# LoRA layer stack on one core: last layers split by token halves, down-weight sums in three steps

## Chip, cores and metric

The kernel runs on one core of one Trainium2 chip. The metric is the time of one execution on the device in microseconds (us); of several executions the median counts. Engines are named as in the profile: PE is TensorE's matrix multiply, PEld its weight load, DVE is VectorE, ACT ScalarE, POOL GpSimd, SP SyncE. A name such as "SPq" means that the engine only issues a DMA there. L446 is line 446 of the kernel before.

## What is computed

Four layers follow one another, each added to its own input. All numbers are fp32; x has 8 x 256 tokens of width 1024.

```python
x = x + L0(x)   # x W^T + b + 2 * (x A^T) B, one adapter for each sequence, rank 16
x = x + L1(x)   # down(silu(gate(x)) * up(x)), hidden width 2752; gate, up and down
                # each add 0.5 * (input A^T) B^T of the sequence's adapter, rank 16
x = x + L2(x)   # (x B^T) A^T, one adapter for each sequence, rank 16
x = x + L3(x)   # (x B^T) A^T, one adapter for each sequence, rank 16
```

The adapters are picked by index inputs, so their tables are gathered by indirect DMAs. L2 and L3 have no dense product. They are computed together here: their two rank-16 products are one "shrink" to ranks and one "expand" back.

## The kernel before

**Layout.** x is held transposed: 1024 features down the partitions, in 8 chunks of 128 (`NC`), and 2048 tokens across. Tokens are worked on in two blocks (`blk` 0 and 1) of 1024, and each block in two halves of 512 (`n` = 0 and 1).

**Products.** A dense product is cut into 2 x 2 blocks and computed by seven products instead of eight (Winograd's form of Strassen's method, `ORDER` 1, 2, 3, 5, 6, 7, 4). In gate, up and the first part of down this is done at two levels. The price is sums: of weights (four for a 2 x 2 set) and of tokens, made by POOL and DVE, and of results, added by DVE out of PSUM. A 128 x 512 fp32 matmul is recorded as two passes.

**Order.** The program is a list of `Unit`s; a unit is one of the outer seven products (or one column of layer 0 or of down). A unit calls `at(slot)` between its inner products. Whatever has been hooked to that slot is emitted there, and after it pieces of a `beside` queue up to a share in cost. A scheduler then keeps for each engine the order so made, as far as data allow. So "slot 4 of unit 2" is a place in every engine's queue.

**Stages.** Layer 0 runs for block 0 and then for block 1. Then each block runs gate and up (`gate_up`), the down projection and the last layers.

- *Layer 0* (units of `job(o)`, four for a block): `sum_w(o)` lets DVE make four sums of the weights (`weight_sums`, L366 to L369) in slot 3 of the unit before. Results are added by DVE with the bias (`with_bias`, L841) and without (`more`, L846).
- *gate_up*: a group `g` of hidden columns is a `Quads` of seven units. POOL makes the outer sums (`outer`, L437) and, a unit ahead, the inner sums `sw` (`inner_sums`, L446 to L449). DVE adds each result bank (`first` L507, `more` L510, and `whole` L519, which adds two SBUF operands). Tokens `tk` are loaded on SP from `toks` a unit ahead (L425).
- *Sums of down weights*: `sum_down(c)` (L755 to L766) treats one of eight pieces of the down weights: load on POOL's DMA queue into `wo` (L759), four POOL sums in place (L761 to L764), four stores to `wsum` in DRAM on POOL's queue (L766). Piece 0 is emitted in block 1's third unit of layer 0 (slot 6), pieces 1 and 2 in the fourth (slot 0), pieces 3 to 7 in block 0's gate_up, in units 2 and 5 of each group (slot 4).
- *Down*: first a `Quads`-like part that reads `wsum`, then four units `2_{blk}_{o}`, whose `job` makes products 1, 5, 6, 3, 2, 7 and leaves product 4 in `pending`, to be emitted by the next `flush()`. DVE adds each to the result `x2` (L1268).
- *Last layers*: `shrink23` multiplies two feature chunks of `x2` as they get ready by the gathered tables `b2` and `b3`. There are four column groups of 32 (`r`, two for a token half and two for the layers), all into one PSUM bank `p23`; `shrink_into` is L261. When the last two chunks are in, `rank_out` (L254) scales and masks the bank into `t`, `expand` (L276) multiplies `t` by `a23`, 64 rows for a token half, and an add puts the result on `x2` (L1392). In block 1, for the chunks in `TAIL` and the second half, ACT copies the bank to `spare` and POOL adds it (L1390). The result is stored (L1396).

**PSUM.** The pools are `ps_a` (2 banks), `ps_b` and `ps_c` (1 each) and `ps_l` (4).

Of the kernel before, what the change touches and what calls it, by code (L numbers as in the profile page):

```python
# [8 lines left out]
F32 = mybir.dt.float32  # L9
# [4 lines left out]
P = 128  # L14
D = 1024
NC = D // P
HC = NC // 2
# [5 lines left out]
TB = 1024  # L23
BB = TB // S
NBLK = NB * S // TB
NN = TB // 512
# [21 lines left out]
TAIL = (0, 2, 4, 6)  # L48
# [6 lines left out]
def kernel(  # L55
# [48 lines left out]
    nc = tc.nc  # L104
# [146 lines left out]
    def rank_out(ps, scale, name):  # L251

        t = tpool.tile([P, 512], F32, tag="t", name=name)
        nc.vector.scalar_tensor_tensor(t, ps, scale, mask, op0=ALU.mult, op1=ALU.mult)  # L254
# [19 lines left out]
    def expand(ps, b, i, t, lo, hi, start=False):  # L274

        nc.tensor.matmul(  # L276
            ps,
            b[lo:hi, i * P : (i + 1) * P],
            t[lo:hi, :],
            start=start,  # L280
            stop=True,
            skip_group_check=True,
        )

    def copy(dst, src, scale=1.0):
        nc.scalar.activation(dst, src, AF.Identity, scale=scale)  # L286
# [6 lines left out]
    class Unit:  # L293


        def __init__(self, name, emit, share):
            self.name, self.emit, self.share = name, emit, share
            self.ahead = []
            units.append(self)
# [5 lines left out]
        def at(self, slot, f):  # L305
            self.ahead.append((0, slot, f))
# [50 lines left out]
    def flush():  # L357
        while pending:
            pending.pop(0)()
# [12 lines left out]
    def product(ps, w, moving, j, start=False):  # L372

        for k, (v, m) in enumerate(zip(w, moving)):
            nc.tensor.matmul(  # L375
                ps,
                v[j],
                m[j],
                start=start and k == 0,
                stop=k == len(moving) - 1,  # L380
                skip_group_check=True,
            )


    class Quads:
# [366 lines left out]
    ]  # L752
    wsum = dram.tile([4, P, 2 * BIG], F32, tag="wsum", name="wsum")

    def sum_down(c):  # L755

        t = big(f"wo_{c}").rearrange("p (j c) -> p j c", j=4)
        cols = slice(c * 512, (c + 1) * 512)
        nc.gpsimd.dma_start(out=t, in_=wd2[:, :, cols].rearrange("j p c -> p j c"))  # L759
        a11, a12, a21, a22 = (t[:, j] for j in range(4))  # L760
        nc.gpsimd.tensor_add(a22, a21, a22)  # L761
        nc.gpsimd.tensor_sub(a21, a11, a21)
        nc.gpsimd.tensor_sub(a11, a22, a11)
        nc.gpsimd.tensor_sub(a12, a12, a11)  # L764
        for j, x in enumerate((a22, a11, a21, a12)):
            nc.gpsimd.dma_start(out=wsum[j, :, cols], in_=x)  # L766

    sts = [{} for _ in range(NBLK)]
    arrival = [c + h for c in range(HC) for h in (0, HC)]
# [2 lines left out]
    def layer0(blk):  # L772
# [149 lines left out]
        for i, o in enumerate((0, 2, 1, 3)):  # L922
            if blk == 0 and i == 0:
                u = Unit("0_plain", lambda at, o=o: plain(o, at), 0)
                u.before(1, 0, load_x)
                for c in range(HC):
                    u.before(1, 0, lambda c=c: sum_x(c))
            else:
                u = Unit(f"0_{blk}_{o}", lambda at, o=o: job(o, at), 1.3)
                u.before(1, 0, lambda o=o: load_w(o))  # L930
                u.before(1, 3, lambda o=o: sum_w(o))
                if i == 0:
                    u.before(1, 0, load_x)
                    for c in range(HC):
                        u.before(1, 4 + c // 2, lambda c=c: sum_x(c))
                    u.at(4, first_shrink)
            if i % 2:
                u.at(8, lambda kk=o % 2: finished(kk))
            if blk == 1 and i > 1:
                for c in ((0,), (1, 2))[i - 2]:  # L940
                    u.at((6, 0)[i - 2], lambda c=c: sum_down(c))

    def gate_up(blk):
        st = sts[blk]
# [38 lines left out]
        def job(g):  # L983
# [86 lines left out]
            q = Quads(blk, f"1_{blk}_{g}", 2, raw, done, SHARE)  # L1070
            q.units[0].before(3, 0, lambda: tables(g))
            if blk == 0 and g < KQ:
                for s, c in ((2, 2 * g + 3), (5, 2 * g + 4)):
                    if c < 8:
                        q.units[s].at(4, lambda c=c: sum_down(c))

        def rest():

# [89 lines left out]
    def down_projection(blk):  # L1168
# [93 lines left out]
        def job(o, at):  # L1262
            p = o + HC
            w, moving = st["wt", o], st["hm"]
            n = f"2_{blk}_{o}"

            def more(k, j, ps):
                nc.vector.tensor_add(x2[k][j], x2[k][j], ps)  # L1268

            at(0)  # L1270
            pa, pc = bank(ps_a, f"pa_{n}"), bank(ps_c, f"pc_{n}")
            product(pa, w, moving, 1, True)
            more(o, 0, pa)
            at(1)
            product(pc, w, moving, 5, True)
            more(p, 1, pc)
            at(2)
            flush()
            at(3)
            product(pa, w, moving, 6)  # L1280
            more(o, 1, pa)
            at(4)
            product(pc, w, moving, 3)
            more(o, 1, pc)
            at(5)
            pb = bank(ps_b, f"pb_{n}")
            product(pb, w, moving, 2, True)
            more(o, 0, pb)
            at(6)
            product(pa, w, moving, 7)  # L1290
            more(p, 1, pa)
            at(7)

            def last():
                product(pa, w, moving, 4)
                more(p, 0, pa)

            pending.append(last)
# [49 lines left out]
        def shrink23(chunks):  # L1348

            for mh in range(2):  # L1350
                for n in range(NN):
                    need(("x2", blk, mh, n))
            need(("b3", blk))
            if chunks[0] == 0:
                st["p23"] = bank(ps_l, f"p23_{blk}")
            for c in chunks:
                for r in range(4):
                    shrink_into(
                        st["p23"],
                        r,  # L1360
                        (st["b2"], st["b3"])[r % 2],
                        NC,
                        c,
                        r // 2,
                        st["x2"][c][r // 2],
                        c == 0,
                        c == NC - 1,
                    )

        def table_a():  # L1370
            st["a23"] = gather_b(a23, off_23[:, blk : blk + 1], f"a23_{blk}")

        def last_layers():
            flush()
            x2 = st["x2"]
            shrink23([HC - 1, NC - 1])
            ps = st["p23"]
            t = rank_out(ps, 1.0, f"t23_{blk}")
            late = []
            if blk + 1 == NBLK:  # L1380
                spare = big("spare").rearrange("p (j t) -> p j t", j=4)
            for o in range(NC):
                pss = [bank((ps_l, ps_a)[o % 2], f"p23_{blk}_{o}_{n}") for n in range(NN)]
                for n in range(NN):
                    expand(pss[n], st["a23"], o, t, 64 * n, 64 * n + 64, start=True)
                for n in range(NN):
                    if blk + 1 == NBLK and o in TAIL and n == 1:

                        copy(spare[:, TAIL.index(o)], pss[n])
                        nc.gpsimd.tensor_add(x2[o][n], x2[o][n], spare[:, TAIL.index(o)])  # L1390
                    else:
                        nc.vector.tensor_add(x2[o][n], x2[o][n], pss[n])  # L1392
                    at = blk * TB + n * 512

                    def store(o=o, n=n, at=at):
                        (nc.scalar, nc.sync)[blk + 1 == NBLK].dma_start(  # L1396
                            out=outT[o * P : (o + 1) * P, at : at + 512], in_=x2[o][n]
                        )


                    if blk + 1 < NBLK:
                        beside.append((0.2, store))
                    elif o in TAIL and n == 1:
                        late.append(store)
                    else:
                        store()
            for f in late:
                f()

        def next_tokens(kk):  # L1410

# [185 lines left out]
```

## Time and profile before

| what | us |
|---|---|
| median of 3 runs (lowest, highest) | 1844.57 (1839.25, 1848.33) |
| the profiled execution, its own time | 1823.64 |
| its span in the trace | 1821.8 |
| mean granted TensorE clock in it | 0.993 of full speed |

The profiled execution is shorter than the median of the runs. A sum made from durations of the profile is compared with 1823.64, and then carried over to the median.

The profile's costliest groups of instructions show what the engines do. The columns are line, engine, operation, output and inputs, size and count, then the busy time and the mean of one in ns, then the engine's idle time just before, and what ended most of it:

```profile
L446 POOL TENSOR_TENSOR sw<-w_B 128x512 f32<-128x512 f32 x60 | 76.8, 1280 | 139.1 <-PE pa L476 121.3
...
L437 POOL TENSOR_TENSOR w_B<-w_B,w_B 128x1024 f32<-128x1024 f32 x40 | 93.5, 2361 | 2.4 <-PE pa L476 2.4
```

A POOL sum of 128 x 512 numbers takes 1.28 us, one of 128 x 1024 takes 2.36. The eight pieces of `wo` are listed by tile: operation, count, the durations in ns (lowest, median, highest) and the starts of the first and the last:

```profile
L766 POOL DMA_DIRECT2D wsum<-wo x32: 540/547/575, 186.8 to 523.3; - x32
L759 POOL DMA_DIRECT2D wo<-in_wd_dram x8: 753/782/797, 173.2 to 505.6; - x8
L761 POOL TENSOR_TENSOR wo<-wo x8: 1263/1271/1276, 183.2 to 516.6; 128x512 f32<-128x512 f32 x8
...
  DMA wo<-in_wd_dram: 22.0, 6
```

The last of these lines says how long POOL stood idle, in six of the eight pieces, until the piece's own load had landed. And this is the end of the chain that ended last (start, duration, what):

```profile
1800.67 1.92 PE p L261 x14
1802.59 0.02 issue
1802.61 0.70 DVE t L254
1803.31 0.04 issue
1803.36 2.90 PE p L276 x12
...
1809.41 1.28 POOL c_d_Y L1390
```

The last shrinks end at 1802.6, DVE makes `t`, and the expands begin at 1803.36.

### The profile page before, as it was taken

The page shows a single profiled execution, that of the slowest core. Times are in us where ns is not written, and L with a number is a line of the kernel's source. Part 1 is how long each engine was busy: PE and PEld are TensorE (multiplying, and loading weights), DVE is VectorE, ACT ScalarE, POOL GpSimd, SP SyncE. Part 2 cuts the span into 40 slices and gives each one's busy share as a digit, 9 for nine tenths or more (in the row PEclk, how much of TensorE's full clock was granted, in tenths as well). Part 3 has the DMA queues.
Part 4 walks back from the last instruction along what each step waited for, and adds up shares of the span by engine and source line. Part 5 has one row for each costly group of instructions (what it writes and reads, how often), then busy time and mean ns, then how long its engine had stood idle before and what let it go on. Part 6 is the DMA issues. An engine that isn't in the chain of part 4 may idle for free.

```text
span 1821.8 us, 20670 instructions
## 1 busy us (share of the span) xinstructions
PE 1797.6 (99%) x7664; PEld 1315.5 (72%) x7664; DVE 1073.0 (59%) x1673; ACT 298.9 (16%) x536; POOL 1006.3 (55%) x778
## 2 busy tenths in 40 slices
PE   9999999999999999999999999999999999999997
PEld 4444477878787878788864568888888887888743
DVE  5484355666757575766852474757575658445623
ACT  0121022021111111133210031120202121221000
POOL 6202578887887677353450467676767664443301
PEclk9999999999999999999999999999999999999999
DMA  6477694767575756679941775575757565655302
GB/s 231 177 278 273 216 369 178 295 217 303 207 309 191 270 188 245 220 280 334 325 143 52 268 299 186 180 276 189 271 193 270 191 239 189 242 174 178 118 0 92
DMA packets 115253, 403.37 MB, mean 221 GB/s; under 512 B 11858, under 2 KB 42706, under 8 KB 105682
## 3 DMA queue, kind: packets, MB, share of 16 engines
q1 hardware_dynamic: 100496, 366.51, 55.4%
q0 software_dynamic: 10496, 28.72, 4.6%
q10 hardware_dynamic: 4162, 6.82, 1.2%
q8 instruction: 62, 1.02, 0.2%
q14 instruction: 37, 0.30, 0.0%
HBM read 317.59 MB, written 84.41 MB: 221 GB/s over the span
## 4 chain that ended last, share of the span: by engine, by line
PE 93%; DVE 5%; DMA 1%; issue 1%; POOL 0%; ACT 0%; POOLq 0%; ACTq 0%; DVEq 0%
PE pa L476 26%; PE pc L476 13%; PE pa_d L476 11%; PE pa L375 10%; PE pb L476 6%; PE pc_d L476 5%; PE pc L375 5%; PE pb_d L476 3%; PE pa_r L476 3%; PE pb L375 3%; PE pl L974 2%; PE pc_r L476 1%; PE pd L261 1%; PE pp L866 1%; PE p L261 1%; DVE c_Z L519 1%
## 5 line engine op out<-in xcount | busy, mean ns | idle before, releaser
L476 PE MATMUL pa<-tk,sw 128*128 128x256 f32 x1120 | 269.6, 384 | 1.7 <-DVE c_X L507 1.7
L476 PE MATMUL pc<-tk,sw 128*128 128x256 f32 x1120 | 268.4, 383 | 0.0
L476 PEld LDWEIGHTS pa<-tk,sw 128*128 128x128 f32 x1120 | 209.5, 190 | 58.7 <-issue 13.7
L476 PEld LDWEIGHTS pc<-tk,sw 128*128 128x128 f32 x1120 | 215.1, 192 | 31.6 <-issue 1.0
L476 PE MATMUL pa<-tk,w_B 128*128 128x256 f32 x960 | 228.4, 381 | 1.5 <-DVE c_Y L510 1.5
L476 PEld LDWEIGHTS pa<-tk,w_B 128*128 128x128 f32 x960 | 181.2, 190 | 36.2 <-DVE c_E L507 6.5
L446 POOL TENSOR_TENSOR sw<-w_B 128x512 f32<-128x512 f32 x60 | 76.8, 1280 | 139.1 <-PE pa L476 121.3
L614 POOL TENSOR_TENSOR dx_d<-dw_d 128x1024 f32<-128x1024 f32 x14 | 33.0, 2359 | 163.9 <-PE pa L476 44.3
L476 PE MATMUL pb<-tk,w_B 128*128 128x256 f32 x480 | 113.9, 380 | 0.0
L476 PE MATMUL pa_d<-dh_d,dw_d 128*128 128x256 f32 x448 | 102.2, 379 | 0.0
L476 PE MATMUL pc_d<-dh_d,dw_d 128*128 128x256 f32 x448 | 101.7, 379 | 0.0
L476 PEld LDWEIGHTS pb<-tk,w_B 128*128 128x128 f32 x480 | 91.8, 191 | 12.7
L507 DVE TENSOR_TENSOR c_X<-c_X,pa 128x512 f32<-128x512 f32 x90 | 61.3, 681 | 63.9 <-PE pa L476 63.8
L437 POOL TENSOR_TENSOR w_B<-w_B,w_B 128x1024 f32<-128x1024 f32 x40 | 93.5, 2361 | 2.4 <-PE pa L476 2.4
L476 PEld LDWEIGHTS pa_d<-dh_d,dw_d 128*128 128x128 f32 x448 | 85.0, 190 | 12.4 <-issue 0.8
L476 PEld LDWEIGHTS pc_d<-dh_d,dw_d 128*128 128x128 f32 x448 | 85.0, 190 | 12.4 <-issue 0.8
L448 POOL TENSOR_TENSOR sw<-w_B 128x512 f32<-128x512 f32 x60 | 85.4, 1423 | 0.0
L449 POOL TENSOR_TENSOR sw<-w_B,sw 128x512 f32<-128x512 f32 x60 | 81.6, 1360 | 3.6
L447 POOL TENSOR_TENSOR sw<-sw,w_B 128x512 f32<-128x512 f32 x60 | 78.9, 1315 | 0.0
L286 ACT ACTIVATE c_X<-pa 128x512 f32<-128x512 f32 x30 | 17.8, 592 | 365.0 <-PE pa L476 365.0
L231 POOL DMA_INDIRECT ad<-in_ad_dram,off_a x48 | 46.0, 958 | 29.2 <-PE pd L261 18.6
L375 PE MATMUL pa<-ht,wd 128*128 128x512 f32 x128 | 59.1, 594 | 0.0
(380 smaller groups left out, 3168.9 us busy)
## 6 DMA issues: line engine op xcount, KB each, us to landing
tk<-toks SPq DMA_DIRECT2D x140, 896.0 KB, 6.7
w_B<-in_wgu_dram SPq DMA_DIRECT2D x40, 1024.0 KB, 5.1
tk_r<-toks SPq DMA_DIRECT2D x28, 896.0 KB, 11.4
hk<-c_Z SPq DMA_DIRECT2D x32, 512.0 KB, 4.3
dh_d<-hk SPq DMA_DIRECT2D x14, 1024.0 KB, 9.3
hk<-c_Y SPq DMA_DIRECT2D x24, 512.0 KB, 3.7
x1d<-x SPq DMA_DIRECT2D x8, 1024.0 KB, 6.0
wo<-in_wd_dram POOLq DMA_DIRECT2D x8, 1024.0 KB, 8.3
```

Of the source, the lines that this page charges most:

```text
L231: nc.gpsimd.indirect_dma_start(out=t, out_offset=None, in_=table, in_offset=bass.IndirectOffsetOnAxis(ap=off, axis=0),)
L261: nc.tensor.matmul(ps[32 * r : 32 * r + 32, :], v, src, start=start, stop=stop, skip_group_check=True)
L375: nc.tensor.matmul(ps, v[j], m[j], start=start and k == 0, stop=k == len(moving) - 1, skip_group_check=True,)
L437: f(self.raw[out][:, c], self.raw[a][:, c], self.raw[b][:, c])
L446: nc.gpsimd.tensor_add(s1, m21, m22)
L447: nc.gpsimd.tensor_sub(s2, s1, m11)
L448: nc.gpsimd.tensor_sub(s3, m11, m21)
L449: nc.gpsimd.tensor_sub(s4, m12, s2)
L476: nc.tensor.matmul(ps[:, q, :], w(j, q, kk), tok(j, kk), start=start and q == 0 and kk == 0, stop=kk == self.deep - 1, skip_group_check=True,)
L507: nc.vector.tensor_add(view(out, r, k), view(old, r, k), ps)
L614: nc.gpsimd.tensor_sub(s3, a11, a21)
L974: nc.tensor.matmul(ps[outs], st["bgu", g][rows, table, n, cols], st["t"][rows, table, n, :], start=True, stop=True, skip_group_check=True,)
```

## The change

1. `sum_down` becomes a class with three steps that are hooked separately. Load and stores go to SP's DMA queue; the four sums stay on POOL, with the same arithmetic.
2. The pieces are placed anew. Pieces 0 to 3 are all in the fourth unit of layer 0's block 1, sums in slots 0, 2, 4 and 6, the load two slots ahead and the store three slots behind. Piece g + 4 is in group g (0 to 3) of block 0's gate_up: load in slot 0 and sums in slot 5 of unit 2, stores in slot 0 of unit 4.
3. In down's `job` product 7 is emitted before product 2.
4. The shrink bank `p23` becomes two banks, one for each token half. The last layers of the second half (its last shrinks, ranks and first expand) are emitted before `flush()`, that is before the last unit's product 4 (which `flush()` emits; it changes only the first half). Then the expands alternate between the halves. `rank_out` is replaced here by two multiplies of 64 rows with the mask.
5. In block 1 the four stores that follow POOL's adds go to ACT's DMA queue, the other twelve stay on SP's.

```diff
-    def sum_down(c):
-
-        t = big(f"wo_{c}").rearrange("p (j c) -> p j c", j=4)
-        cols = slice(c * 512, (c + 1) * 512)
-        nc.gpsimd.dma_start(out=t, in_=wd2[:, :, cols].rearrange("j p c -> p j c"))
-        a11, a12, a21, a22 = (t[:, j] for j in range(4))
-        nc.gpsimd.tensor_add(a22, a21, a22)
-        nc.gpsimd.tensor_sub(a21, a11, a21)
-        nc.gpsimd.tensor_sub(a11, a22, a11)
-        nc.gpsimd.tensor_sub(a12, a12, a11)
-        for j, x in enumerate((a22, a11, a21, a12)):
-            nc.gpsimd.dma_start(out=wsum[j, :, cols], in_=x)
+    class SumDown:
+        def __init__(self, c):
+            self.c, self.cols = c, slice(c * 512, (c + 1) * 512)
+        def load(self):
+            self.t = big(f"wo_{self.c}").rearrange("p (j c) -> p j c", j=4)
+            nc.sync.dma_start(out=self.t, in_=wd2[:, :, self.cols].rearrange("j p c -> p j c"))
+        def sums(self):
...
+        def store(self):
+            for j, x in enumerate((3, 0, 2, 1)):
+                nc.sync.dma_start(out=wsum[j, :, self.cols], in_=self.t[:, x])
...
-            if blk == 1 and i > 1:
-                for c in ((0,), (1, 2))[i - 2]:
-                    u.at((6, 0)[i - 2], lambda c=c: sum_down(c))
+            if blk == 1 and i == 3:
+                for c in range(4):
+                    w = SumDown(c)
+                    u.at(2 * c - 2 if c else 0, w.load)
+                    u.at(2 * c, w.sums)
+                    u.at(2 * c + 3, w.store)
...
             if blk == 0 and g < KQ:
-                for s, c in ((2, 2 * g + 3), (5, 2 * g + 4)):
-                    if c < 8:
-                        q.units[s].at(4, lambda c=c: sum_down(c))
+                w = SumDown(g + 4)
+                q.units[2].at(0, w.load)
+                q.units[2].at(5, w.sums)
+                q.units[4].at(0, w.store)
...
+            product(pa, w, moving, 7)
+            more(p, 1, pa)
+            at(6)
             pb = bank(ps_b, f"pb_{n}")
             product(pb, w, moving, 2, True)
             more(o, 0, pb)
-            at(6)
-            product(pa, w, moving, 7)
-            more(p, 1, pa)
             at(7)
...
             for c in chunks:
-                for r in range(4):
-                    shrink_into(
...
+                for n in range(NN):
+                    shrink_half(c, n)
+
+        def shrink_half(c, n):
+            if c == 0:
+                st["p23", n] = bank(ps_l, f"p23_{blk}_{n}")
+            for j, b in enumerate((st["b2"], st["b3"])):
+                shrink_into(
+                    st["p23", n], 2 * n + j, b, NC, c, n, st["x2"][c][n], c == 0, c == NC - 1
+                )
...
+            def ranks(n):
+                rows = slice(64 * n, 64 * n + 64)
+                t[n] = tpool.tile([P, 512], F32, tag="t", name=f"t23_{blk}_{n}")
+                nc.vector.tensor_mul(t[n][rows], st.pop(("p23", n))[rows], mask[rows])
+
+            def store(o, n):
+                at = blk * TB + n * 512
+                queue_of = nc.sync if final and not (n == 1 and o in TAIL) else nc.scalar
+                queue_of.dma_start(out=outT[o * P : (o + 1) * P, at : at + 512], in_=x2[o][n])
+
+            def products(*which):
+                pss = []
+                for o, n in which:
+                    banks.append(None)
+                    ps = bank((ps_l, ps_a)[len(banks) % 2], f"p23_{blk}_{o}_{n}")
+                    expand(ps, st["a23"], o, t[n], 64 * n, 64 * n + 64, start=True)
+                    pss.append(ps)
+                for (o, n), ps in zip(which, pss):
+                    if final and n == 1 and o in TAIL:
+
+                        copy(spare[:, TAIL.index(o)], ps)
+                        nc.gpsimd.tensor_add(x2[o][n], x2[o][n], spare[:, TAIL.index(o)])
+                        late.append((o, n))
+                        continue
+                    nc.vector.tensor_add(x2[o][n], x2[o][n], ps)
...
+            for c in (HC - 1, NC - 1):
+                shrink_half(c, 1)
+            shrink_half(HC - 1, 0)
+            ranks(1)
             flush()
-            x2 = st["x2"]
-            shrink23([HC - 1, NC - 1])
-            ps = st["p23"]
-            t = rank_out(ps, 1.0, f"t23_{blk}")
...
+            products((0, 1))
+            shrink_half(NC - 1, 0)
+            products((1, 1))
+            ranks(0)
+            products((2, 1))
+            for o in range(NC - 3):
+                products((o, 0), (o + 3, 1))
+            for o in range(NC - 3, NC):
+                products((o, 0))
             for f in late:
-                f()
+                store(*f)
```

More of the change, by code (lines that the diff above doesn't have):

```diff
@@ L753 @@
     wsum = dram.tile([4, P, 2 * BIG], F32, tag="wsum", name="wsum")
-    def sum_down(c):
-        t = big(f"wo_{c}").rearrange("p (j c) -> p j c", j=4)
-        cols = slice(c * 512, (c + 1) * 512)
-        nc.gpsimd.dma_start(out=t, in_=wd2[:, :, cols].rearrange("j p c -> p j c"))
-        a11, a12, a21, a22 = (t[:, j] for j in range(4))
-        nc.gpsimd.tensor_add(a22, a21, a22)
-        nc.gpsimd.tensor_sub(a21, a11, a21)
-        nc.gpsimd.tensor_sub(a11, a22, a11)
-        nc.gpsimd.tensor_sub(a12, a12, a11)
-        for j, x in enumerate((a22, a11, a21, a12)):
-            nc.gpsimd.dma_start(out=wsum[j, :, cols], in_=x)
+    class SumDown:
[5 more added lines that the diff above has]
+        def sums(self):
+            a11, a12, a21, a22 = (self.t[:, j] for j in range(4))
+            nc.gpsimd.tensor_add(a22, a21, a22)
+            nc.gpsimd.tensor_sub(a21, a11, a21)
+            nc.gpsimd.tensor_sub(a11, a22, a11)
+            nc.gpsimd.tensor_sub(a12, a12, a11)
+        def store(self):
+            for j, x in enumerate((3, 0, 2, 1)):
+                nc.sync.dma_start(out=wsum[j, :, self.cols], in_=self.t[:, x])
     sts = [{} for _ in range(NBLK)]
@@ L1353, in shrink23 @@
             need(("b3", blk))
-            if chunks[0] == 0:
-                st["p23"] = bank(ps_l, f"p23_{blk}")
             for c in chunks:
-                for r in range(4):
-                    shrink_into(
[L1359 to L1368, printed above, removed]
+                for n in range(NN):
[7 more added lines that the diff above has]
+                )
         def table_a():
@@ L1373, in last_layers @@
         def last_layers():
-            flush()
-            x2 = st["x2"]
-            shrink23([HC - 1, NC - 1])
-            ps = st["p23"]
-            t = rank_out(ps, 1.0, f"t23_{blk}")
[L1379 to L1406, printed above, removed]
@@ new lines, in last_layers @@
+            x2, t, late, banks = st["x2"], {}, [], []
+            final = blk + 1 == NBLK
+            if final:
+                spare = big("spare").rearrange("p (j t) -> p j t", j=4)
+            def ranks(n):
[6 more added lines that the diff above has]
+                queue_of.dma_start(out=outT[o * P : (o + 1) * P, at : at + 512], in_=x2[o][n])
@@ new lines, in products @@
+            def products(*which):
[12 more added lines that the diff above has]
+                    nc.vector.tensor_add(x2[o][n], x2[o][n], ps)
+                    if final:
+                        store(o, n)
+                    else:
+                        beside.append((0.2, lambda o=o, n=n: store(o, n)))
```

## The prediction

> **What bounds the kernel now.** I read the busy times first, then who TensorE waits for, then two windows that run the same program, then single instructions inside them.
>
> ```profile
> span 1821.8 us, 20670 instructions
> PE 1797.6 (99%) x7664; PEld 1315.5 (72%) x7664; DVE 1073.0 (59%) x1673; ACT 298.9 (16%) x536; POOL 1006.3 (55%) x778
> ```
>
> TensorE is the bound: 1821.8 - 1797.6 = 24 us are all that it idles, start and tail included. The change takes no product away, so it can win only from those idle times, from slowed passes, and from the tail. TensorE's list of waits names them:
>
> ```profile
> PE pa L375 <- DVE x L841: 2.9, 1, 2.9
> PE pa L476 <- DVE c_X L507: 1.7, 2, 0.8
> PE pa L476 <- DVE c_X L510: 1.6, 1, 1.6
> PE pa L476 <- DVE c_Y L510: 1.5, 2, 1.0
> ...
> PE p L276 <- DVE t L254: 0.8, 1, 0.8
> ```
>
> All are waits for VectorE. Gate and up run the same program for both blocks, but only block 0 holds five of the eight sum_down pieces. Both windows (busy time of PE, PEld, DVE, ACT, POOL; granted clock; DMA) start and end at the same instructions:
>
> ```profile
> 280.00:568.00 288.00, 283.57 (x1314) 229.47 (x1313) 192.22 (x266) 42.66 (x74) 234.66 (x179) 0.99 0.67 247
> 1076.50:1355.50 279.00, 279.00 (x1314) 227.73 (x1313) 173.37 (x265) 42.74 (x74) 190.05 (x133) 0.99 0.61 217
> ```
>
> Block 0 takes 9 us longer for the same 1314 matmuls; set against the same pd shrink in both blocks (363.08 and 1159.19 us, and so on) the difference is 8.8 us. DVE is busy 19 us longer with one instruction more. The timelines show why: DVE, then POOL, in block 0; then DVE at the same place of block 1.
>
> ```profile
> 361.00 4.11 DVE L519 TENSOR_TENSOR c_Y<-c_Y,c_X 128x512 f32<-128x512 f32 x1
> ```
> ```profile
> 359.74 1.08 POOL L766 DMA_DIRECT2D wsum<-wo  x2
> 360.83 1.28 POOL L446 TENSOR_TENSOR sw<-w_B 128x512 f32<-128x512 f32 x1
> 362.05 1.28 POOL L448 TENSOR_TENSOR sw<-w_B 128x512 f32<-128x512 f32 x1
> 363.27 1.27 POOL L447 TENSOR_TENSOR sw<-sw,w_B 128x512 f32<-128x512 f32 x1
> ```
> ```profile
> 1158.19 0.69 DVE L519 TENSOR_TENSOR c_Y<-c_Y,c_X 128x512 f32<-128x512 f32 x1
> ```
>
> L519 reads two operands from SBUF. It lasts until POOL pauses after three sums: 4.11 instead of 0.69 us. The pa bank is then added late (L507, L510) and TensorE waits. Layer 0 shows the same on block 1's last weights:
>
> ```profile
> 182.60 2.46 DVE L366 TENSOR_TENSOR sw<-w 128x512 f32<-128x512 f32 x1
> 185.10 2.34 DVE L367 TENSOR_TENSOR w<-w 128x512 f32<-128x512 f32 x1
> 187.47 1.75 DVE L368 TENSOR_TENSOR sw<-w 128x512 f32<-128x512 f32 x1
> 189.26 1.74 DVE L369 TENSOR_TENSOR sw<-w,sw 128x512 f32<-128x512 f32 x1
> 190.92 0.74 DVE L841 SCALAR_TENSOR_TENSOR x<-pa,bias,x 128x512 f32<-128x512 f32 x1
> ```
>
> Near 156 to 159 us, with POOL quiet, the same four take 0.68 to 0.69 us each.
>
> **What the Trainium skill says.** The page "SBUF — State Buffer", section "SBUF: two separate sides", says that DVE and GpSimd share one port pair as an exclusive lock held for a whole instruction, taken by a DVE op with two SBUF inputs against a GpSimd op that reads SBUF. The trace agrees: only L519 and L366 to L369 swell (to 4.79 us at 426.32), while L507 and L510, with one operand in PSUM, stay at 0.67. The same page warns of descriptors for POOL-queue DMAs, which GpSimd writes itself: here 0.55 us of POOL for a store, 0.78 for a load. "TensorE: Matmul & The Clock Gate", Part 1, says that TensorE drops to half clock after an idle window: after the 1.5 us wait at 462.58 eight 256-column passes ran 0.43 instead of 0.215 us. "TensorEngine Tiling (Array Packing)", "Key Properties", says that a switch of tile mode drains the array: a row-group pass after a 128-row one starts 0.52 instead of 0.43 us later.
>
> **The change part by part.**
>
> *Pieces 0 to 3, layer 0.* Before, piece 0's four POOL ops (183.23 to 190.44) meet the four DVE sums of the last unit's weights, and TensorE stands from 188.60 to 191.71: 3.1 us. After, the first load goes out on SP behind the x1d stores, about 177; a 1 MB load took 8.3 us, so POOL starts no earlier than 185.3. The DVE sums start at 182.60, and 4 x 0.69 ends them at 185.4. In the last unit DVE has only operations with a PSUM operand (L841, L846), so four pieces of 4 x 1.28 us cost nothing there. POOL must be free again for a gather that TensorE's expand releases near 227; the last piece ends near 219. Gain 3.1. If the load lands 3 us sooner, half the stall stays.
>
> *Pieces 4 to 7, gate and up of block 0.* Before, five pieces 3 to 7 stand in POOL's order, and each holds POOL for a 10 us load of its own, then 4 x 1.28 us of sums and (4 x 0.55 + 0.78) us of descriptors. Thereafter POOL is late and does L446 to L449 without pauses. The offset between the blocks shrinks by 2.57, 1.31, 4.13 and 0.76 us over the pieces near 331, 361, 426 to 463 and 524: 8.8 in sum. After, each group holds one piece: its load leaves SP in unit 2's slot 0, 8 to 10 us ahead of the sums, and all descriptors leave POOL. The pieces in unit 5, which caused the 4.11 and 4.13 us L519s, go: that is all of 2.57 and 4.13. A piece in unit 2 still moves POOL's next chain (sw_5) back by up to 5.1 us; group 3 shows POOL free at 615 where TensorE tolerates 2.7 us. I take 0.2 to 0.3 a group, 1.0 in all: gain 7.8. Bounds: 8.8 (nothing left) and 5 (1 us lost in every group).
>
> *SP's queue* now waits in place for POOL's sums before four stores of 0.25 MB. Behind them stand toks loads: in group 0 the load that was issued at 301.5 goes at about 316.5, lands 7 to 11 us later, and is needed at 334: 7 us to spare. Groups 1 to 3 have their stores after the sums by unit 4. Cost 0.
>
> *Product 7 ahead of product 2* in the down job: same passes; its bank comes from ps_a, free two products earlier. 0.
>
> *Last layers, block 0.* Before, 1004.12 to 1027.68 (23.6 us) are set by 16 DVE adds at 0.60 us each start to start and their PSUM banks. After, half the expands come earlier, but 8 shrink steps instead of 6 stand at the end (2 x 0.43 us), 20 expand passes in alternating order, and no rest product is drawn in between. DVE's end moves from 24.1 to 23.7 us, TensorE's next work is later: +0.9 (from -0.3 to +1.5).
>
> *Last layers, block 1.* Before, TensorE ends the last product, waits 0.81 us for t (L254), expands from 1803.36 to 1811.64; 16 stores leave SP until 1816.25, and land 0.65 us apart. The span ends at 1821.8, 1.3 us after the last landing (1820.3). After, with the durations of before: first half's shrink at 1796.8, the first expand at 1802.7, adds from 1803.7; the four POOL adds (copy 0.6, add 1.3, store 0.7 on ACT, one after another, 2.6 us each) delay one bank, so the last DVE add comes at 1814.9 instead of 1812.4. But SP issues 12, not 16, and has the last out at 1815.4; 16 landings of 0.65 from the first, at 1808, end at 1818.5. Gain 1.8. Bounds: 2.8 (landings follow issues) and 0.5 (ACT's stores are late by one POOL add).
>
> Sum: -3.1 - 7.8 + 0.9 - 1.8 = -11.8. From the profiled execution's 1823.6 that makes 1811.8; the median of the runs, 1844.6, lies 21 us above the profile, and the stalls removed are counted in us, so I take the same 11.8 from it: **1832.7**.
>
> **Rivals.**
> A, the sum above: 1832.7.
> B, POOL's chain still starves L519 in each group: the one piece moves sw_5's sums under the L519s of unit 3, at 1.31 us a group as the piece near 361 cost, 5.2 in all. For it: L519 at 331.66 starts within 0.5 us of L446 at 331.2. Against: group 0's piece at unit 2 cost much less than that at unit 5. -11.8 + 4.2 = -7.6: about 1837.
> C, shrinks that write two PSUM banks no longer run four at a time. If the two banks' column groups ran one after the other, each of six shrinks a block (two steps of 0.43 us) would take twice its 0.86 us, in 2 blocks: +10.3, that is 1843. For it: no such pair stands in the trace. Against: row-group expands into two banks start within 7 ns of each other.
> D, slower: SP's stores hold the toks loads. In each group SP stands until POOL has summed. It decides once POOL's sums end more than 7 to 11 us later than worked out, for instance if POOL falls behind the gathers; then each group waits some 6 us for its tokens, 24 us in all, net +12: 1857. For it: SP issues everything that TensorE reads. Against: the margins above.
>
> **How the numbers follow.** A 0.70, B 0.14, C 0.08, D 0.08. What a measurement can tell from no change is 0.5%, 9.2 us, so faster means below 1835.4. A's bounds, summed loosely, are 1827 to 1838, 6 of 7 below 1835.4: 0.60; B adds a third of 0.14, in all 0.66 with a little for A's good end. D is slower: 0.08. The rest is 0.26. The range runs from 1824 to 1845: A and B whole, C's middle, D left out.
>
> **What would show it.** Right: no TensorE wait for L841's successor near 188; the four sums of weights at 0.7 us; block 0's gate and up within 1 or 2 us of 279; no L519 above 3 us there; wo and wsum gone from the software queue; no wait for t at the end; the last store landing 4 us or less after the last DVE add. Wrong: TensorE waits that name tk loads (D); p23 shrinks that start 0.2 us or more apart in a step (C); L519 at 2 to 4 us in every group (B).

## The result, and the profile after

| | median, us | runs |
|---|---|---|
| before | 1843.33 (1834.63 to 1851.87) | 18 |
| after | 1833.85 (1828.80 to 1837.16) | 18 |

The ratio is 0.9948, with a 95% interval from 0.9934 to 0.9962: about 9.6 us faster (7.0 to 12.2). The forecast was 1832.7.

The profiled execution of after, however, is longer than that of before: its span is 1831.3 us against 1821.8. So the two traces must be set against each other stage by stage. TensorE's list of waits in after (total us, times, longest) shows the reason at its head:

```profile
PE t L261 <- issue: 13.6, 9, 2.2
PE pa L476 <- DVE c_X L507: 1.7, 2, 0.8
...
PE p L276 <- ACT spare L286: 0.7, 2, 0.4
```

The waits for x, for c_X and c_Y of L510, for td and for t are gone. In their place stands 13.6 us in layer 0's very first shrink, which the change does not touch. TensorE's timeline of after there (start, duration, instructions, the idle time before them) and two windows of the same stretch (busy time of PE, PEld, DVE, ACT, POOL; granted clock; DMA share; GB/s):

```profile
34.59 1.94 PE L261 MATMUL t<-x,a 128*32 128x512 f32 x11
37.04 0.59 PE L261 MATMUL t<-x,a 128*32 128x512 f32 x1 [0.52 <-issue]
39.14 0.59 PE L261 MATMUL t<-x,a 128*32 128x512 f32 x1 [1.51 <-issue]
41.94 1.01 PE L261 MATMUL t<-x,a 128*32 128x512 f32 x1 [2.21 <-issue]
```
```profile
36.50:40.94 4.44, 1.20 (x3) 0.27 (x2) 0.00 (x0) 0.00 (x0) 3.40 (x4) 1.00 0.08 15
40.95:58.00 17.05, 6.73 (x7) 0.82 (x6) 0.00 (x0) 0.00 (x0) 10.38 (x11) 0.50 0.14 38
```

The granted clock from 36 to 58 us is 0.61 on average, the steps start 2.1 and 2.8 us apart, and the trace shows no engine or transfer that is waited for. The clock did not begin it: for the first 4.4 us, with the steps already that far apart, the granted clock is still 1.00, and it is 0.50 only from 40.95 on. In before the whole shrink took 3.7 us (34.46 to 38.1). To take this out, the same TensorE instructions of two traces are matched by tile and order, and the difference of their starts, taken before and after a stage, gives what the stage gained or lost. Minus is faster than the profiled execution of before:

| stage, us | after | after_third | sums_only | last_only | block0_whole | stores_shared | before_again |
|---|---|---|---|---|---|---|---|
| start, first shrink of layer 0 | +24.2 | -0.1 | -0.7 | -0.2 | -0.5 | -0.9 | +0.4 |
| layer 0, last unit | -3.2 | -3.2 | -3.2 | -1.6 | -3.2 | -3.2 | -1.7 |
| small rest group, block 0 | -2.5 | -2.6 | +0.1 | -0.6 | +0.3 | +0.1 | 0.0 |
| gate and up, block 0 | -8.8 | -8.8 | -8.8 | +0.6 | -8.8 | -8.8 | -3.0 |
| last layers, block 0 | +1.3 | +1.2 | 0.0 | +1.3 | 0.0 | 0.0 | 0.0 |
| small rest group, block 1 | +0.1 | +0.1 | -3.3 | +0.1 | -1.7 | -3.3 | +1.7 |
| tail | -1.6 | -1.5 | -0.4 | +0.8 | -1.4 | -0.9 | 0.0 |
| span, all in all | +9.5 | -14.8 | -16.3 | +0.4 | -15.2 | -16.9 | -2.5 |

(The other columns are runs told of below; after_third is the kernel after once more, before_again the kernel before once more.) For layer 0, DVE in after at the place where before showed 1.7 to 2.5 us:

```profile
206.79 0.68 DVE L366 TENSOR_TENSOR sw<-w 128x512 f32<-128x512 f32 x1
207.51 0.69 DVE L367 TENSOR_TENSOR w<-w 128x512 f32<-128x512 f32 x1
208.24 0.69 DVE L368 TENSOR_TENSOR sw<-w 128x512 f32<-128x512 f32 x1
208.96 0.69 DVE L369 TENSOR_TENSOR sw<-w,sw 128x512 f32<-128x512 f32 x1
```

And both blocks' gate and up in after, as windows:

```profile
298.50:577.80 279.30, 279.30 (x1319) 227.63 (x1320) 174.48 (x267) 44.25 (x76) 211.70 (x148) 1.00 0.67 242
1088.40:1367.40 279.00, 279.00 (x1314) 227.75 (x1313) 172.68 (x263) 41.62 (x72) 189.66 (x134) 0.99 0.61 216
```

Block 0 now costs what block 1 costs, and PE is busy in all of it. DVE's 192 us of before are 174. The longest L519 of 512 columns lasts 1.33 us; before it was 4.79.

### The profile page after: what moved, and what is told of

Its sections match the earlier page's. It is cut to its first block, busy times and chain, and to the rows that moved or that the text cites. A ratio compares the mean times of both kernels' runs of the same rounds, so it can differ in the third digit from the quotient of the medians.

```text
span 1831.3 us, 20664 instructions
## 1 busy us (share of the span) xinstructions
PE 1805.3 (99%) x7664; PEld 1313.0 (72%) x7664; DVE 1053.3 (58%) x1675; ACT 298.9 (16%) x536; POOL 981.3 (54%) x738
## 4 chain that ended last, share of the span: by engine, by line
PE 95%; DVE 3%; issue 1%; DMA 0%; ACT 0%; POOL 0%; ACTq 0%; DVEq 0%; POOLq 0%
PE pa L476 26%; PE pc L476 13%; PE pa_d L476 11%; PE pa L375 10%; PE pb L476 6%; PE pc_d L476 5%; PE pc L375 5%; PE pb_d L476 3%; PE pa_r L476 2%; PE pb L375 2%; PE pl L986 2%; PE pp L875 2%; PE pd L261 1%; PE pc_r L476 1%; PE p L261 1%
## 5 line engine op out<-in xcount | busy, mean ns | idle before, releaser
L231 POOL DMA_INDIRECT ad<-in_ad_dram,off_a x48 | 45.6, 951 | 27.0 <-PE pd L261 16.9
```

The source lines that it names most:

```text
L231: nc.gpsimd.indirect_dma_start(out=t, out_offset=None, in_=table, in_offset=bass.IndirectOffsetOnAxis(ap=off, axis=0),)
```

## The experiments

**Is the start part of the change?** The kernel before once more, without an edit.

> The kernel before, once more. Two theories on the first 60 us, where the trace of after shows TensorE at a granted clock of 0.61 for 22 us and that of before does not. (1) The slow start is a matter of the single execution, whatever the kernel: then this trace can have it too, at the same shrink of layer 0, and its spans lie near 1822 without it and near 1822 + 24 = 1846 with it. (2) The change brings it: then this trace has none, and all spans lie near 1822. The rest of the trace, from 62 us on, should repeat that of before within 1 us under both: waits of 3.1 us near layer 0's last unit, and 288 us for block 0's gate and up against 279 for block 1's.

It ran in 1820.42 us (14 runs; 1.0007 of the kernel before, interval 0.9989 to 1.0025), with a span of 1819.3 and no slow start. So the question of the start can't be settled from this run alone. What was expected of the rest of the trace did not come. TensorE's wait for the add with the bias in layer 0 is 1.3 us and not 2.9, and block 0's gate and up is 3.0 us shorter than in the first trace of before:

```profile
PE pa L375 <- DVE x L841: 1.3, 1, 1.3
```

So the stalls of before differ from one execution to the next. Three traces have the old sums: before, before_again and last_only below. In layer 0 they lose 3.2, 1.6 and 1.7 us against the kernels with the new sums, in block 0's gate and up 8.8, 5.8 and 9.4. A gain taken from one of them is the price of that one execution.

The kernel after was run on two chips, again without edit (on which chip the result itself was measured is not known):

> The kernel after, once more, on a chip where the kernel before had no slow start in its traces. Theory: the start is no part of the change, so the change gains here what the parts gave, 12 us (3.2 layer 0, 8.8 gate and up, minus 1.3 block 0's last layers, plus 1.5 tail), spread over 10 to 14 by the clock in the small rest groups. Rival: the change itself makes the start slow, then 22 us of granted clock 0.61 near 36 us again.

> The kernel after beside stores_shared on one chip. Theory: on a chip without the slow start it gains 12 us, on one with it 7 to 10, as before; in both the trace from 62 us on has no wait of TensorE in layer 0 and none for c_X or c_Y above 1 us in gate and up.

| chip | before, median | after, median | ratio, 95% interval | slow start in the traces |
|---|---|---|---|---|
| 10 | 1842.13 | 1834.71 | 0.9960, 0.9945 to 0.9976 | in all four taken |
| 1 | 1820.34 | 1809.91 | 0.9940, 0.9921 to 0.9960 | in none of four |
| 11 | 1820.05 | not run | | in none of four |

All four traces from chip 10 are of kernels with the change or most of it, and show 23 to 25 us lost at the start; after_third, the same program on chip 1, shows none. The kernel before also lies 21.8 us higher on chip 10 than on chip 1. So the start goes with the chip and not with the change, as far as the medians of before can stand for a trace. In the profiled execution of before it is missing, while its medians, 1843 to 1845, lie where chip 10's do. After lost 24.8 us from chip to chip and before 21.8; where those 3 us are is open, as no trace of before was taken on a chip with the slow start. What makes a chip start slowly is open too.

**Which half of the change has the gain?** Two kernels, each with one part alone.

```diff
 sums_only: before, and only
-    def sum_down(c):
+    class SumDown:            # load, sums, store; its places in layer 0 and gate_up
 last_only: before, and only
+            product(pa, w, moving, 7)   # ahead of product 2, shrink_half, last_layers
```

> Only the new sums of down weights (three steps, four pieces in layer 0, SP's queue); the last layers as before. Theory: this part has all of the gain, 3.2 us in layer 0 and 8.8 in block 0's gate and up, so from 62 us on it gains 12.0, and L519 never lasts 3 us there. Block 0's gate and up takes 279 to 280 us. Rival: the gain in gate and up comes of TensorE's clock in one execution, not of L519; then this trace keeps waits of 1 to 2 us for c_X and c_Y in block 0. Time: 9 to 13 us below the kernel before.

> Only the last layers by halves, the product order in down and the four stores on ACT's queue; the sums of down weights as before. Theory: block 0's last layers lose 1.3 us, the tail wins 1.5, together no change (within 1 us); the waits of layer 0 and of gate and up stay. Rival: the halves win in both blocks, 3 us or more.

sums_only ran in 1807.73 us, before beside it in 1820.05: ratio 0.9940, interval 0.9921 to 0.9960. The table shows -3.2 and -8.8 in the two stages named. last_only ran in 1823.53, ratio 1.0017, interval 1.0002 to 1.0032: the last layers by halves, alone, are a loss of 3.5 us in the medians (0.4 to 5.8), where no change within 1 us was expected. The waits of L510 stay in it:

```profile
PE pa L476 <- DVE c_X L510: 2.4, 1, 2.4
...
PE pa L476 <- DVE c_Y L510: 1.6, 2, 1.0
```

So the sums of down weights have all of the gain, and the rival (a clock of one execution) falls: the five traces with the new sums in the table show -8.8 in gate and up, to 0.01 us the same, while the three with the old sums all lie 5.8 us or more above them.

last_only's tail is 0.8 us slower than before where the same code in after is 1.6 faster. Both move the output at about 390 GB/s for most of the last 9 us of their traffic, but after's span ends 1 us after the last 0.5 us in which DMA moved anything, last_only's 4. What stands between is POOL's last DRAIN, an instruction at the end of the program. The view of its line gives the durations of the three DRAINs there (ns: lowest, median, highest) and the starts of the first and the last. In this order: before, last_only, own_wait (told of below), after:

```profile
L1592 POOLq DRAIN  x3: 46/97/9732, 1811.3 to 1821.5; - x3
L1607 POOLq DRAIN  x3: 46/97/9723, 1811.7 to 1822.0; - x3
L1622 POOLq DRAIN  x3: 46/97/6298, 1795.7 to 1803.7; - x3
L1620 POOLq DRAIN  x3: 40/102/5152, 1823.2 to 1831.0; - x3
```

The long one starts with POOL's last add. It takes 9.72 to 9.73 us in the four traces whose eight loads and thirty-two stores of down weights are on POOL's queue (before, before_again, last_only, pool_queue), 6.30 in own_wait, which has four of the loads there, and 5.14 to 5.15 in the nine that have none. So its length goes with what was issued on POOL's queue. In last_only it ends at 1821.44, 2.44 us after SP's DRAIN at that place, and the span ends 0.79 us later; in after SP's ends last. An estimate from these traces: with SP last, last_only's span would end 2.5 us earlier, and its tail would be the -1.6 of after. In before too POOL's DRAIN ends after SP's, by 0.45 us.

**Do the halves pay in block 0?**

```diff
 block0_whole: after, and
+        shrink23 = shrink23_halves if blk else shrink23_whole
-        units[-1].at(9, last_layers)
+        units[-1].at(9, last_layers_halves if blk else last_layers_whole)
+            if blk:                       # product 7 ahead of 2 in block 1 alone
+                seventh()
```

> The kernel after, but block 0's last layers and the product order of its down job as before; block 1 keeps the halves. Theory: block 0 is bound there by sixteen adds of 0.60 us, so the halves only bring more TensorE steps: 1.3 us come back, so this lies 1 to 1.5 us below after. Rival: the loss in block 0 is only moved work of the next block, then no difference.

It took 1808.43 us (ratio 0.9939, interval 0.9918 to 0.9959), and the 1.3 us are back: 0.0 against before in that stage. The time can't show it, as after did not run beside it; the matched traces do. The rival, work moved into the next block, falls with it. TensorE in after's block 0:

```profile
1025.02 1.12 PE L276 MATMUL p<-t,a 64*128 64x512 f32 x2
1026.07 1.08 PE L261 MATMUL p<-c_d_X,bb 128*32 128x512 f32 x4
1027.08 9.53 PE L276 MATMUL p<-t,a 64*128 64x512 f32 x30
1036.54 1.13 PE L476 MATMUL pa_r<-tk_r,w_r_B 128*128 128x256 f32 x4
```

TensorE has no gaps, but its expands go at the pace of DVE's sixteen adds, 0.60 us each in both kernels, and the rest products (pa_r), two groups of which filled gaps in before, begin only after them.

**What made POOL late in gate and up?** Before, three things stood together: the load on POOL's queue right ahead of the sums, the stores' descriptors on POOL, and pieces in unit 5. Three kernels put back one or two each.

```diff
 pool_queue: after, and
-            nc.sync.dma_start(out=self.t, in_=wd2[...])
+            nc.gpsimd.dma_start(out=self.t, in_=wd2[...])
-                nc.sync.dma_start(out=wsum[j, :, self.cols], in_=self.t[:, x])
+                nc.gpsimd.dma_start(out=wsum[j, :, self.cols], in_=self.t[:, x])
 old_places: after, and
+                for s, c in ((2, 2 * g + 3), (5, 2 * g + 4)):    # pieces 4 to 7
+                        q.units[s].at(0, w.load)
+                        q.units[s].at(5, w.sums)
+                        (q.units + [None])[s + 1].at(3, w.store)
 own_wait: as old_places, but
+                        q.units[s].at(4, lambda w=w: w.load(nc.gpsimd))
+                        q.units[s].at(4, w.sums)
```

> The kernel after with the loads and stores of the down weights back on POOL's queue, at the new places and in the three steps. Theory (the place and the early load decide): POOL pays 0.78 + 4 x 0.55 = 3 us more for each piece, but never waits for its own load; TensorE loses less than 1 us in layer 0 and 0 to 3 us in gate and up, so within 3 us of after. Rival (POOL's descriptors decide): 5 us or more of the 8.8 come back, with L519 of 3 us and over in block 0.

> The kernel after, with pieces 4 to 7 back at the places of before in gate and up (units 2 and 5 of the groups: piece 4 in group 0's unit 5, 5 and 6 in group 1, 7 in group 2), but load in slot 0, sums in slot 5, stores in the next unit, all DMAs on SP. Theory (POOL's wait for its own load made it late): with the load ahead POOL is late by 5.1 us only, and TensorE loses 0 to 3 us against after. Rival (unit 5 itself is the wrong place, as DVE has there the L519s of product 7): pieces 4 and 6 cost 2.6 and 4.1 us again, 6 us and more together.

> The kernel after with pieces 4 to 7 at the places of before (units 2 and 5) and their loads again on POOL's queue right ahead of the sums; the stores stay on SP. Theory (POOL stands until its own load lands, falls behind and then sums without pauses beside L519): POOL waits 7 to 9 us four times, L519 lasts 3 us and more again, TensorE waits in gate and up come back, 4 to 8 us in all. Rival: the wait is nothing and the stores' descriptors on POOL made it late; then TensorE loses less than 1 us.

In gate and up all three gain the full 8.8 us: none of the expected losses came. old_places ran in 1834.45 us, as after beside it (1834.71). own_wait (one execution, 1806.06) shows POOL still standing for its load,

```profile
344.36 1.28 POOL L767 TENSOR_TENSOR wo<-wo 128x512 f32<-128x512 f32 x1 [4.16 <-DMA wo<-in_wd_dram]
```

but the longest L519 is 1.77 us. So the descriptors alone are not enough (pool_queue), nor unit 5 (old_places), nor unit 5 and the wait for the own load together (own_wait). By these three runs the loss of before needs the descriptors and at least one of the other two, or the fifth piece, number 3, that stood in group 0 and that no run put back. Which, was not tried.

pool_queue as a whole is a miss for the theory: 1846.57 us, 11.9 above after beside it; against before the ratio is 1.0020 (1.0009 to 1.0030), slower. The time went in layer 0 and the rest group, which I had put at less than 1 us:

```profile
PE pc_r L476 <- POOL sw_r L449: 5.7, 1, 5.7
```
```profile
241.03 1.10 POOL L775 DMA_DIRECT2D wsum<-wo  x2
247.10 1.27 POOL L767 TENSOR_TENSOR wo<-wo 128x512 f32<-128x512 f32 x1 [4.97 <-DMA wo<-in_wd_dram]
```

With four pieces in one unit POOL stands for the loads that it issues itself (4.97 us here) and for sixteen stores, and the sums of the next weights, sw_r, come late. TensorE loses 9.7 us between layer 0 and gate and up. So SP's queue is what makes room for four pieces in layer 0; in gate and up it is not needed once there is one piece in a group.

**Does POOL make DVE's sums slow in layer 0?** First piece 0's sums were put back to their old slot:

```diff
 piece0_early: after, and
+            if blk == 1 and i == 2:
+                w = SumDown(0)
+                u.at(1, w.load)
+                u.at(6, w.sums)
+                u.at(7, w.store)
```

> The kernel after, with piece 0's sums back in slot 6 of layer 0's third unit of block 1 (load in slot 1, stores in slot 7, both on SP). Theory (POOL's four sums meet DVE's four sums of weights, and each makes the other wait): DVE's L366 to L369 last 1.3 us and more each, and TensorE waits 1 to 3 us for the add with the bias near there. Rival (POOL's descriptors between its sums made the wait in the kernel before): with SP's queue no wait of TensorE above 0.3 us.

This told nothing: SP issued the load at 201.6 behind the x1d stores, as in after, so POOL's sums began at 211.06, past DVE's four (207.21 to 210.07). The time was 1835.76 us. Then four POOL adds were put where they had to meet them:

```diff
 lock_probe: after, and
+                def probe(o=o):
+                    x, rest = x1(o + HC, 1), st["sw", o][:, 1536:]
+                    for _ in range(4):
+                        nc.gpsimd.tensor_add(rest, x, x)
+                u.at(2, probe)
```

> The kernel after with four more POOL adds of 128x512 in layer 0's third unit of block 1, reading what DVE has just written and writing to a part of a buffer that nothing reads, so that they start with DVE's four sums of the last weights. Theory (two SBUF operands against a POOL operation): DVE's L366 to L369 go from 2.8 us in all to 5 and more, the add with the bias comes late, TensorE waits 2 to 5 us there. Rival (POOL's descriptors between its sums were needed to make the wait): DVE's sums keep their 0.69 us.

DVE and then POOL in lock_probe:

```profile
182.38 0.68 DVE L366 TENSOR_TENSOR sw<-w 128x512 f32<-128x512 f32 x1
183.09 1.41 DVE L367 TENSOR_TENSOR w<-w 128x512 f32<-128x512 f32 x1
184.54 1.41 DVE L368 TENSOR_TENSOR sw<-w 128x512 f32<-128x512 f32 x1
185.98 1.41 DVE L369 TENSOR_TENSOR sw<-w,sw 128x512 f32<-128x512 f32 x1
187.32 0.74 DVE L851 SCALAR_TENSOR_TENSOR x<-pa,bias,x 128x512 f32<-128x512 f32 x1
```
```profile
182.54 5.75 POOL L954 TENSOR_TENSOR sw<-x 128x512 f32<-128x512 f32 x4 [14.47 <-DVE x L851]
```

The sums of two SBUF operands that meet a POOL add take 1.41 us each instead of 0.69; L851, with an operand in PSUM, keeps its 0.74. So the exclusion is shown. But the four take 5.0 us here and not the 8.4 of before (182.60 to 191.0), and TensorE waits for nothing, where 2 to 5 us were expected. What before has in addition are POOL's DMA issues. POOL in before at that place, then DVE and POOL in pool_queue, where the issues are back:

```profile
183.23 1.27 POOL L761 TENSOR_TENSOR wo<-wo 128x512 f32<-128x512 f32 x1
184.83 0.75 POOL L759 DMA_DIRECT2D wo<-in_wd_dram  x1 [0.33 <-issue]
185.60 1.28 POOL L762 TENSOR_TENSOR wo<-wo 128x512 f32<-128x512 f32 x1
186.80 0.57 POOL L766 DMA_DIRECT2D wsum<-wo  x1
187.38 1.29 POOL L763 TENSOR_TENSOR wo<-wo 128x512 f32<-128x512 f32 x1
```
```profile
206.58 1.93 DVE L367 TENSOR_TENSOR w<-w 128x512 f32<-128x512 f32 x1
```
```profile
206.68 1.27 POOL L767 TENSOR_TENSOR wo<-wo 128x512 f32<-128x512 f32 x1
208.03 1.61 POOL L768 TENSOR_TENSOR wo<-wo 128x512 f32<-128x512 f32 x1
```

A DVE sum that was held ends 0.55 to 0.57 us after the end of the POOL add that it met, in before, in lock_probe and in pool_queue alike. It makes no difference whether a store's issue follows that add (before: L762 ends at 186.88, L367 at 187.44) or another add does (pool_queue: L767 ends at 207.95, L367 at 208.51). So the issue behind an add does not hold the sum. The issues count because they stretch POOL's string: DVE gets one sum through for each POOL add, and the adds end 1.8 to 2.4 us apart in before, with a load or a store issued between, against 1.4 in lock_probe. Two of before's four, L366 and L367, also began while POOL was still issuing a load, 0.5 to 0.6 us ahead of the add that they then waited for. So both theories hold a part: the adds hold DVE's sums, and the issues between them stretch the time. In pool_queue the three that met POOL took 1.93, 1.64 and 1.78 us, and TensorE waited 0.7.

**A version with both gains.** The new sums, the old last layers, and the output's stores on two queues:

```diff
 stores_shared: sums_only, and
-                        (nc.scalar, nc.sync)[blk + 1 == NBLK].dma_start(
+                        (nc.scalar, nc.sync)[blk + 1 == NBLK and o % 2 == 0].dma_start(
```

> The new sums of down weights with the last layers of before in both blocks; in block 1 the eight stores of the odd chunks go out on ACT's queue, the other eight on SP's. Theory: the expands end 2.4 us earlier behind the last product than in the kernel after, block 0 loses nothing (1.3 us), and with two queues the last store leaves SP about 2 us after the last add, so the span's end comes 2 to 4 us earlier than in the kernel after. Rival: the landings, 0.65 us apart, set the end and not the issues; then it lies within 1.5 us of the sums alone and of after.

Beside after on chip 1: 1806.68 us (1805.93 to 1809.60) against 1809.91 (1806.75 to 1811.45), six runs each. Against before it is 0.9928, interval 0.9908 to 0.9947; after has 0.9940. It is the fastest median here, though the intervals overlap. 1.2 us of it are block 0's last layers. The tail is not better than after's: -0.9 against -1.5, so the theory's 2 to 4 us did not come, and the rival, which expected no more than 1.5 us of the stores, was right there. The spans of the two traces differ by 2.1 us; what is not these two stages is the clock in the small rest groups and the start.

## Why the prediction was right, and where it was not

The forecast was 11.8 us, the measured difference 9.6 (7.0 to 12.2 by the interval). The stages that the change touches sum to -3.2 - 8.8 + 1.3 - 1.6 = -12.3 against the one trace that the prediction was made from. With the mean stalls of the three traces of the old sums (2.1 in layer 0, 8.0 in gate and up) an estimate of the sum is -10.4, nearer to what was measured.

- *Pieces 0 to 3, layer 0*: put at -3.1, measured -3.2 against that trace, -1.6 against before_again. The place is right, and so is the mechanism, POOL's add against DVE's sum; what it leaves out is that the DMA issues between POOL's adds stretch the stall, from the 5.0 us of lock_probe to the 8.4 of before.
- *Pieces 4 to 7, gate and up*: put at -7.8 with a bound at -8.8; measured -8.8 in every run with the new sums, and -5.8 against before_again. The term mis-sized is the 1.0 us taken for the piece that stays in each group: it costs nothing. The sum says that each piece holds POOL for a load of 10 us; by the 22.0 us in six pieces shown above it stood 3.7 us on average. The sentence that pieces in unit 5 caused the 4.1 us L519s does not stand as put: pieces in unit 5 without POOL's store issues cost nothing either.
- *SP's queue*: put at 0, and no wait of TensorE names a tk load. Rival D falls.
- *Last layers, block 0*: put at +0.9, measured +1.2 to +1.3; the range given reached +1.5.
- *Last layers, block 1*: put at -1.8, measured -1.6 and -1.5. The size is in part luck. The term counted only landings, and these won 1.1 us (the last one at 1820.29 in before; at 1805.91 in after_third, whose matched instructions lie 13.3 us earlier). The other 0.45 us come from POOL's DRAIN, which ended last in before and no longer does; the prediction did not have it.
- *Rival B*: L519 stays below 1.4 us in gate and up; it falls. *Rival C*: in after the shrinks of both halves, into two banks, start 0.01 us apart in a step (1800.63 and 1800.64); it falls.
- *What was not in the sum*: two small rest groups in which TensorE's clock differs from execution to execution (block 0's: -2.5 us in after's trace, +0.1 in sums_only's), the start, and the spread of before's own stalls. The prediction noted that the median lay 21 us above the profiled execution, and took the gain over without asking where those 21 us were.

## What to carry to other kernels

When two passes of a loop run the same program and one is longer, match their instructions and take the steps in the offset: each step is a price. But it is the price in one execution: the stalls of the kernel before differed by 1.7 and 3.0 us in the next one, so take a second trace before a step is called a gain. A helper engine is cheap in a gap and dear in a queue; take away one of several delays that add up and the stall can vanish whole, so undo them one by one before naming the one. Look at the DRAINs at the end too: a queue that was used long before can still end last. And when a profiled execution is far from the median of the runs, find out what it lacks before its sum is carried over.

## What the runs showed of the hardware

- A chip can start slowly: on chip 10 the first column-tiled shrink, 3.7 us elsewhere, took 23 to 25 us longer, in four of four traces; on chips 1 and 11 in none of eight. In after's trace the granted clock fell to 0.50 only 4.4 us into the slow stretch.
- After a TensorE wait of 0.6 us the granted clock fell in one trace and not in another. The same wait for trep stands in before and after; in the 9 us behind it the granted clock was 0.81 in before and 1.00 in after. The first line is before's window behind trep, the second after's:

```profile
268.00:277.00 9.00, 8.45 (x26) 5.44 (x27) 7.18 (x15) 3.96 (x6) 3.36 (x3) 0.81 0.94 372
```
```profile
288.90:297.90 9.00, 8.16 (x30) 4.71 (x30) 8.34 (x16) 4.54 (x8) 3.18 (x3) 1.00 1.01 408
```

- The fall of the clock that the prediction puts at 462.58 in before came at 466.5, and the wait ahead of it lasted 1.3 us (463.18 to 464.50), not 1.5.
- A DVE sum of two SBUF operands that meets a POOL add ends some 0.55 us after that add, whatever POOL does next. Of the 623 sums of 128 x 512 on L366 to L369 and L519 that took over 0.9 us in the fourteen traces, 614 ended 0.54 to 0.58 us after an add. How long they took depends on where they began: 1.41 us in lock_probe, up to 2.46 where it began ahead of the add during a load's issue, 4.11 at 361.00, where it waited for three adds. Why it gets through after one add in one place and after three in another was not tested.
- POOL's DRAIN at the end took 9.7 us with eight loads and thirty-two stores on POOL's queue, 6.3 with four loads, 5.15 with neither. All kernels have the same 152 gathers on that queue, and the last load or store on it was issued 1.2 ms or more before the DRAIN.
